# Head-norm reciprocal roots by small VectorE steps, and a Hadamard rotation moved to GpSimd, in a two-layer FFN kernel

## The chip, the cores and the metric

The kernel runs on one core of a Trainium2 chip. The metric is device time in microseconds (us) of one execution, as the median of several runs. One further execution is recorded by the hardware profiler; its page and its trace are what the readings below come from. The engines are TensorE (PE, with its weight loads PEld), VectorE (DVE), ScalarE (ACT), GpSimd (POOL) and SyncE (SP), which here only issues DMAs.

## What is computed

Two layers work on x of shape (128, 32, 256), with a condition of shape (128, 256). Cut to what matters here:

```python
# layer 0: 32 Runge-Kutta steps of a coupled system, driven by x, then an FFN with MX block quantization
def _q_w(w):                       # blocks of 32: shared power-of-two scale, then few-bit elements, at most 6
    return _quantize_mx(w, 2, 1.0, 2.0, 6.0)
...
gate = _mx_linear(x, w_gate); up = _mx_linear(x, w_up)
x = x + _mx_linear(silu(gate) * up, w_down)

# layer 1: attention with 16 heads of 16, then an FFN with rotated, quantized activations
q = q * rsqrt(mean(q * q, axis=-1) + 1e-6) * g_q          # per head
k = k * rsqrt(mean(k * k, axis=-1) + 1e-6) * g_k
attn = softmax((q @ k.T) * d ** -0.5)
...
gate, up = h_bitlinear(h, w_gate), h_bitlinear(h, w_up)   # fwht over 256, 8-bit activations, ternary weights
out = h_bitlinear(silu(gate) * up, w_down)                # fwht over 1024
```

The function fwht is a Walsh-Hadamard transform: log2(n) stages of sums and differences.

## The kernel before

The kernel has two phases. **Phase one** is layer 0. Its unit is one time step of all 128 sequences, so a tile is 128 x 256. `step` does one Runge-Kutta step: matrix products on PE, tanh and squares on ACT, multiply-adds on DVE (L513), cubes on POOL (L569). `ffn0` sends each step's state through quantization, the three MX products and a norm, some steps behind `step`. Before the first `ffn0` can multiply, six halves of weights pass through `mx_weight`: a block maximum, three small instructions for the scales (L627, L632, L639), a multiplication by the inverse scale on POOL (L688), then on DVE a clip to 6 (L692), a mask that keeps the exponent (L695), a lower bound and a factor that make a rounding constant of it (L698), its addition and subtraction, which round (L699, L700), and on POOL the multiplication by the scale (L703). The wide tiles are 128 x 1024.

**Phase two** is layer 1. Its unit is a chunk of 128 tokens, four sequences of 32; `tokens(g)` is called for 32 chunks, and up to seven are on the way at once (`behind`). One chunk does, in order: q, k and v on PE (L1043, L1050); the squares on ACT (L1059) and their sums per head on DVE (L1060); the reciprocal root of 128 x 32 means on POOL, as a multiply-add (L1063) and a power of -0.5 (L1064); the multiplications of q and k by it on DVE (L1069, L1076), and of q by the product of the gains, `g_prod`, on POOL (L1081); attention with transposes and reductions on DVE; a rotation over 256 folded into a matrix (L1151); quantization (`quantum`, L1018 to L1026); gate and up on PE (L1184), Silu on ACT (L1192), the product on DVE (L1199, two halves of 512). Then comes the rotation over 1024. Three of its ten stages, those between the eight blocks of 128 elements, are butterflies: for each stage one instruction for the sums and one for the differences (L1215), two stages on DVE and the third on POOL. The other seven stages are a matrix on PE (L1226), after a transposition (L487). A second quantization and the last product (L1249, L1256) end the chunk.

**The order** is made by a planner. Every piece of work is an item with an engine, an estimated cost, and the tiles that it reads and writes; `Work.order` plans all of them forth and back for 30 rounds from these costs, keeps the best plan, and the instructions of every engine are emitted in that order. Each engine then works through its own list in that fixed order. An item with `port=True` is not planned at the same time as another item with `port=True`: the planner takes DVE and POOL to exclude each other there. The pools of tiles (`tiny`: 24 of 128 x 32; `wide`: 8 of 128 x 1024; four single and two double PSUM banks in phase two) are shared out by the same plan. In `mx_scales` an intermediate lies in PSUM instead of SBUF; the sums of squares and the reciprocal roots lie in `tiny`, in SBUF.

Of the kernel before, what the change touches and what calls it, by code (L numbers as in the profile page):

```python
# [13 lines left out]
I32 = mybir.dt.int32  # L14
AF = mybir.ActivationFunctionType
ALU = mybir.AluOpType
AX = mybir.AxisListType
# [12 lines left out]
EXP_MASK = 0x7F800000  # L30
TINY = 2.0**-124

MAGIC = 12582912.0
HEADS = 16
D_HEAD = 16
EPS_RMS = 1e-6
EPS_QUANT = 1e-5

PE, DVE, ACT, POOL, SP = "PE", "DVE", "ACT", "POOL", "SP"

# [243 lines left out]
def kernel(  # L284
# [22 lines left out]
    nc = tc.nc  # L307
# [26 lines left out]
    mid = slots("mid", HALF, 10)  # L334
    slim = slots("slim", N, 18)
    tiny = slots("tiny", FF // BLOCK, 24)
# [38 lines left out]
    neg_half = tile_of("neg_half", [P, 2 * HEADS])  # L375
# [7 lines left out]
    add = work.add  # L383
# [294 lines left out]
    def mx_weight(w, dst, b_dst, part, rank):  # L678
        raw, rows = load_half(w, part, rank)
        nb = FF // BLOCK  # L680
        amax = Buf(tiny)
        amax_item(amax, lambda a: a, raw, lambda a: a, 1.13, rank)
        scl, inv = mx_scales(amax, nb, rank, 0.5, tiny)
        add(DVE, 0.1, lambda: nc.vector.tensor_scalar(scl.ap, scl.ap, 0.25, None, MULT), [], [scl], rank=rank)
        y, big, wq = Buf(wide), Buf(wide), Buf(wide_bf)
        add(
            POOL, 1.87,
            lambda: nc.gpsimd.tensor_tensor(blocks(y.ap), blocks(raw.ap), spread(inv.ap, BLOCK), MULT),  # L688
            [raw, inv], [y], rank=rank, port=True,
        )  # L690
        ts = nc.vector.tensor_scalar
        add(DVE, 0.6, lambda: ts(y.ap, y.ap, 6.0, -6.0, ALU.min, ALU.max), [], [y], rank=rank, port=True)  # L692

        add(
            DVE, 0.6, lambda: ts(big.ap.bitcast(I32), y.ap.bitcast(I32), EXP_MASK, None, ALU.bitwise_and),  # L695
            [y], [big], rank=rank, port=True,
        )
        add(DVE, 0.6, lambda: ts(big.ap, big.ap, 1.0, MAGIC / 2.0, ALU.max, MULT), [], [big], rank=rank, port=True)  # L698
        add(DVE, 1.135, lambda: nc.vector.tensor_tensor(y.ap, y.ap, big.ap, ADD), [big], [y], rank=rank, port=True)  # L699
        add(DVE, 1.135, lambda: nc.vector.tensor_tensor(y.ap, y.ap, big.ap, SUB), [big], [y], rank=rank, port=True)  # L700
        add(
            POOL, 1.87,
            lambda: nc.gpsimd.tensor_tensor(blocks(wq.ap), blocks(y.ap), spread(scl.ap, BLOCK), MULT),  # L703
            [y, scl], [wq], rank=rank, port=True,
        )
        turn_weight(wq, dst, b_dst, part, rows, rank)
# [68 lines left out]
    def constants_of_phase_two(rank):  # L775

        b_hf, had_ffn = load_fixed("had_ffn", [P, P], had, rank)
        b_qkv, w_qkv_sb = load_fixed("w_qkv_sb", [P, NC, 3 * N], w_qkv.rearrange("(c p) n -> p c n", p=P), rank)
        w_o = load(mid, w_out.rearrange("(c p) n -> p c n", p=P), rank, as_=two)
        b_gq, g_qk_sb = fixed("g_qk_sb", [P, 2, D_HEAD])  # L780
        for n, g in enumerate((g_q, g_k)):
            add(
                SP, 0.45, lambda n=n, g=g: nc.sync.dma_start(g_qk_sb[:, n, :], g.partition_broadcast(P)),
                fills=[b_gq], rank=rank, tail=1.8,
            )
        ts = nc.gpsimd.tensor_scalar
# [12 lines left out]
        add(  # L799
            POOL, 0.3, lambda: nc.gpsimd.tensor_tensor(g_prod, g_qk_sb[:, 0, :], g_qk_sb[:, 1, :], MULT),  # L800
            [b_gq], [b_gp], rank=rank,
        )
        add(POOL, 0.3, lambda: ts(g_prod, g_prod, 1.0, D_HEAD**-0.5, MULT, MULT), [], [b_gp], rank=rank)
        w_oT = Buf(mid)
        for m in range(NC):
            pw = Buf(ps_turn)
            add(PE, 0.22, lambda pw=pw, m=m: turn(pw.ap, two(w_o.ap)[:, m, :]), [w_o], [pw], rank=rank)
            add(
                ACT, 0.33,
                lambda pw=pw, m=m: nc.scalar.copy(two(w_oT.ap)[:, :, m * P : (m + 1) * P], two(pw.ap)),  # L810
                [pw], fills=[w_oT], rank=rank,
            )
# [16 lines left out]
        return b_hf, had_ffn, b_qkv, w_qkv_sb  # L829
# [180 lines left out]
    def heads(ap):  # L1010
        return ap.rearrange("p (h d) -> p h d", d=D_HEAD)

    def quantum(name, src, n, cost, rank):
# [14 lines left out]
        add(DVE, 0.25, scales, [], [am, sc], rank=rank)  # L1028
        return am, sc

    def tokens(g):
        rank = PHASE_TWO + g
        tok = slice(g * P, (g + 1) * P)
# [23 lines left out]
        v_pad, sq, rstd, qn, k_pad = Buf(v_pads), Buf(mid), Buf(tiny), Buf(slim), Buf(k_pads)  # L1057
        add(ACT, 0.26, lambda: nc.scalar.copy(v_pad.ap[:, :, :D_HEAD], heads(pv.ap[:, :N])), [pv], [v_pad], rank=rank)
        add(ACT, 0.477, lambda: nc.scalar.activation(sq.ap, pqk.ap, AF.Square), [pqk], [sq], rank=rank)  # L1059
        add(DVE, 0.6, lambda: nc.vector.tensor_reduce(rstd.ap, heads(sq.ap), AX.X, ADD), [sq], [rstd], rank=rank)  # L1060

        def rsqrt():
            nc.gpsimd.tensor_scalar(rstd.ap, rstd.ap, 1.0 / D_HEAD, EPS_RMS, MULT, ADD)  # L1063
            nc.gpsimd.tensor_tensor(rstd.ap, rstd.ap, neg_half, ALU.pow)  # L1064

        add(POOL, 5.65, rsqrt, [], [rstd], rank=rank)
        add(
            DVE, 0.335,
            lambda: tt(heads(qn.ap), heads(pqk.ap)[:, :HEADS, :], spread(rstd.ap[:, :HEADS], D_HEAD), MULT),  # L1069
# [261 lines left out]
```

## Time and profile before

| what | value |
|---|---|
| time, median of 3 runs | 880.15 us (878.64 to 880.85) |
| the profiled execution: time | 884.23 us |
| the profiled execution: span, first to last instruction | 882.5 us |
| mean granted PE clock | 0.956 |
| phase one, last Runge-Kutta state (L606) | 393.7 us after the span's start |
| phase two, first matmul on q and k (L1043) | about 429 us |
| phase two, first and last product of a chunk (L1199) | 474.2 and 852.3 us |
| POOL's power (L1064) | 32 instructions, 175.1 us |
| DVE's butterflies (L1215) | 128 instructions, 87.9 us |
| POOL's butterflies (L1215) | 64 instructions, 82.1 us |

How to read the lines of the profile: a group names its line in the kernel, its engine, its operation, the tile written and the tiles read, the shapes, and the count; then the busy time in us and the mean duration of one in ns, and then the idle time of the engine just before, with what ended most of it. A line of the timeline begins with the start and the duration in us; "x2" there means two instructions in a row, merged. A line of the waits says who waited for whom: us in total, times, longest.

### The profile page before, as it was taken

Reading aid. Unit: us, or ns where it says so; the run is one execution under the profiler, and the core shown is the slowest. Engines: PE = TensorE matmul, PEld = TensorE weight load, DVE = VectorE, ACT = ScalarE, POOL = GpSimd, SP = SyncE. Lnnn points to the kernel's source line nnn. Section 1 sums busy time; section 2 is a strip of 40 time slices with the busy share of each in tenths; the row PEclk is TensorE's granted clock in tenths of the full one; section 3 lists DMA queues with packets and bytes.
Section 4 is the critical chain, followed back from the end, with each engine's and each line's share of the span. In section 5 each row is a group of like instructions: output and inputs, shape, how many; then the busy total and the mean of one; then the engine's idle time right before and its main releaser. Section 6 shows DMA issues by size and latency. Waiting matters only on the chain. (4 is left out here: it accounts for less than half of the span.)

```text
span 882.5 us, 25579 instructions
## 1 busy us (share of the span) xinstructions
PE 781.6 (89%) x10300; PEld 590.1 (67%) x10300; DVE 749.4 (85%) x1885; ACT 499.3 (57%) x1014; POOL 636.4 (72%) x619
## 2 busy tenths in 40 slices
PE   7788999999999999994678989998999988988974
PEld 4566777778887887872344666866677665766654
DVE  5989999899999999998157978997989769798882
ACT  4243455555665665654324666767677647576653
POOL 5645898878899988799699649658866477766330
PEclk9989999999999999997769999999999989999997
DMA  8211332222322442425200122222122212122132
GB/s 265 66 32 42 71 77 57 71 57 67 70 73 73 106 99 65 105 65 99 47 2 15 24 45 48 64 56 56 19 56 56 55 36 56 37 54 44 47 70 66
DMA packets 128887, 55.49 MB, mean 63 GB/s; under 512 B 102144, under 2 KB 127616, under 8 KB 128768
## 3 DMA queue, kind: packets, MB, share of 16 engines
q1 hardware_dynamic: 128768, 53.85, 26.2%
q8 instruction: 81, 1.33, 0.6%
q14 instruction: 38, 0.31, 0.1%
HBM read 21.32 MB, written 8.39 MB: 34 GB/s over the span
## 5 line engine op out<-in xcount | busy, mean ns | idle before, releaser
L1064 POOL TENSOR_TENSOR tiny<-tiny,neg_half 128x32 f32<-128x32 f32 x32 | 175.1, 5472 | 2.7
L1215 POOL TENSOR_TENSOR wide<-wide 128x512 f32<-128x512 f32 x64 | 82.1, 1300 | 99.7 <-DVE wide L1215 60.8
L562 PEld LDWEIGHTS ps_stage<-slim,coup 128*128 128x128 f32 x1024 | 132.2, 194 | 14.3 <-ACT slim L555 5.2
L562 PE MATMUL ps_stage<-slim,coup 128*128 128x128 f32 x1024 | 138.9, 279 | 0.1
L569 POOL TENSOR_TENSOR slim<-slim,slim 128x256 f32<-128x256 f32 x96 | 73.6, 767 | 37.3 <-ACT slim L556 35.5
L1215 DVE TENSOR_TENSOR wide<-wide 128x512 f32<-128x512 f32 x128 | 87.9, 715 | 0.3
L548 PE MATMUL ps_stage<-drives,eye 128*128 128x256 f32 x256 | 81.2, 400 | 5.3 <-DVE ps_stage L513 3.8
L548 PE MATMUL ps_stage<-slim,eye 128*128 128x256 f32 x256 | 78.0, 394 | 7.6 <-DVE slim L513 7.6
L555 ACT ACTIVATE slim<-slim 128x256 f32<-128x256 f32 x96 | 39.5, 411 | 70.9 <-DVE slim L513 58.3
L1043 PE MATMUL ps_one<-w_qkv_sb,xnT 128*128 128x512 f32 x128 | 69.4, 671 | 2.1 <-DVE coup L1076 0.9
L917 POOL TENSOR_TENSOR wide_bf<-mid,tiny 128x512 bf16<-128x512 fp8e4 x64 | 67.7, 1064 | 3.9 <-DVE mid L841 3.7
L909 POOL TENSOR_TENSOR mid<-mid,tiny 128x512 f32<-128x512 f32 x64 | 66.3, 1049 | 4.1 <-DVE tiny L639 3.7
L1226 PE MATMUL ps_two<-had_ffn,wide 128*128 128x128 f32 x512 | 64.6, 282 | 4.3 <-DVE tiny L1025 1.6
L1226 PEld LDWEIGHTS ps_two<-had_ffn,wide 128*128 128x128 f32 x512 | 61.8, 196 | 8.4 <-DVE tiny L1025 2.1
L548 PEld LDWEIGHTS ps_stage<-slim,eye 128*128 128x128 f32 x256 | 43.5, 193 | 24.1 <-DVE slim L513 15.2
L1128 PEld LDWEIGHTS ps_one<-v_pad,mid 32*32 32x32 f32 x4096 | 42.2, 107 | 25.1 <-issue 15.5
L1199 DVE SCALAR_TENSOR_TENSOR wide<-ps_two,tiny,mid 128x512 f32<-128x512 f32 x64 | 46.5, 737 | 13.1 <-ACT mid L1192 12.9
L1128 PE MATMUL ps_one<-v_pad,mid 32*32 32x17 f32 x4096 | 47.8, 182 | 10.4 <-issue 5.9
L1192 ACT ACTIVATE mid<-ps_two,tiny 128x512 f32<-128x512 f32 x64 | 42.9, 686 | 21.9 <-PE ps_two L1184 21.0
L556 ACT ACTIVATE slim<-slim 128x256 f32<-128x256 f32 x96 | 38.9, 406 | 26.0 <-DVE slim L513 25.8
L1234 ACT ACTIVATE wide<-ps_two,magic,tiny 128x1024 f32<-128x1024 f32 x32 | 38.5, 1202 | 24.6 <-DVE tiny L1026 18.3
L548 PEld LDWEIGHTS ps_stage<-drives,eye 128*128 128x128 f32 x256 | 40.4, 195 | 14.3 <-DVE ps_stage L513 9.0
(153 smaller groups left out, 2065.7 us busy)
## 6 DMA issues: line engine op xcount, KB each, us to landing
x_step<-in_x_dram SPq DMA_DIRECT2D x32, 128.0 KB, 2.3
x_add<-in_x_dram SPq DMA_DIRECT2D x32, 128.0 KB, 2.1
x_dram<-slim SPq DMA_DIRECT2D x32, 128.0 KB, 1.7
slim<-x_dram SPq DMA_DIRECT2D x32, 128.0 KB, 2.2
out_dram<-slim SPq DMA_DIRECT2D x32, 128.0 KB, 1.7
raws<-in_L_ffn_w_gate_dram SPq DMA_DIRECT2D x4, 512.0 KB, 5.0
raws<-in_L_ffn_w_up_dram SPq DMA_DIRECT2D x4, 512.0 KB, 5.6
raws<-in_L_ffn_w_down_dram SPq DMA_DIRECT2D x4, 512.0 KB, 3.6
```

The source lines that it names most:

```text
L548: PE, cost, lambda: nc.tensor.matmul(ps[i].ap, lhsT=eyes[eye], rhs=src.ap, start=False, stop=False),
L562: nc.tensor.matmul(ps[i].ap[:, sl], lhsT=coup[i][:, c, sl], rhs=two(th.ap)[:, c, :], start=False, stop=(c == NC - 1 and m == NC - 1),)
L569: POOL, 0.685, lambda: nc.gpsimd.tensor_tensor(sq.ap, sq.ap, qi.ap, MULT),
L909: lambda it=it, ks=ks: nc.gpsimd.tensor_tensor(blocks(it.ap), blocks(it.ap), spread(binv.ap[:, ks], BLOCK), MULT),
L917: lambda b8=b8, ks=ks, sl=sl: nc.gpsimd.tensor_tensor(blocks(bq.ap[:, sl]), blocks(b8.ap), spread(bscl.ap[:, ks], BLOCK), MULT),
L1043: nc.tensor.matmul(pqk.ap, lhsT=xnT_flat[:, c, tok], rhs=w_qkv_sb[:, c, : 2 * N], start=(c == 0), stop=(c == NC - 1),)
L1064: nc.gpsimd.tensor_tensor(rstd.ap, rstd.ap, neg_half, ALU.pow)
L1128: nc.tensor.matmul(by_v(po.ap)[row, hd, :], lhsT=by_head(exT.ap)[row, hd, :], rhs=v_pad.ap[row, hd, :], start=True, stop=True,)
L1192: lambda pgu=pgu, act=act: nc.scalar.activation(act.ap, pgu.ap[:, :HALF], AF.Silu, scale=sgu.ap[:, 0:1]),
L1199: lambda pgu=pgu, act=act, sl=sl: stt(it.ap[:, sl], pgu.ap[:, HALF:], sgu.ap[:, 1:2], act.ap, MULT, MULT),
L1215: eng.tensor_tensor(dv[:, :, e, :], sv[:, :, 0, :], sv[:, :, 1, :], op)
L1226: nc.tensor.matmul(pfh.ap[:, sl], lhsT=iT.ap[:, sl], rhs=had_ffn, start=True, stop=True)
```

## The change

There are three parts.

The reciprocal root of the heads' mean squares no longer runs on POOL. A new function `rsqrt` does it in nine DVE instructions on `tiny` tiles of 128 x 32: a multiply-add, a first guess from the float's bits, and two polishing passes of three and four instructions. The result comes out with a constant factor, `RSQRT`, which `g_prod` takes out again. Each chunk uses four `tiny` tiles for this instead of one. In the planner each of the nine steps costs 0.1 and has no `port` mark.

The three butterfly stages of the rotation over 1024 all go to POOL (six instructions for each chunk instead of two).

In `mx_weight` the clip at the start goes; the mask takes one more bit by an OR in the same instruction; the first of the two rounding passes becomes a subtraction on POOL, and the second a custom DVE addition that saturates at 6 and -6 (`TENSOR_ADD_SAT`, which `step` already uses).

```diff
         ts = nc.vector.tensor_scalar
-        add(DVE, 0.6, lambda: ts(y.ap, y.ap, 6.0, -6.0, ALU.min, ALU.max), [], [y], rank=rank, port=True)
-
-        add(
-            DVE, 0.6, lambda: ts(big.ap.bitcast(I32), y.ap.bitcast(I32), EXP_MASK, None, ALU.bitwise_and),
+
+        add(
+            DVE, 0.6,
+            lambda: ts(big.ap.bitcast(I32), y.ap.bitcast(I32), EXP_MASK, 1 << 22, ALU.bitwise_and, ALU.bitwise_or),
             [y], [big], rank=rank, port=True,
         )
-        add(DVE, 0.6, lambda: ts(big.ap, big.ap, 1.0, MAGIC / 2.0, ALU.max, MULT), [], [big], rank=rank, port=True)
-        add(DVE, 1.135, lambda: nc.vector.tensor_tensor(y.ap, y.ap, big.ap, ADD), [big], [y], rank=rank, port=True)
-        add(DVE, 1.135, lambda: nc.vector.tensor_tensor(y.ap, y.ap, big.ap, SUB), [big], [y], rank=rank, port=True)
+        add(DVE, 0.6, lambda: ts(big.ap, big.ap, 1.5, 2.0**22, ALU.max, MULT), [], [big], rank=rank, port=True)
+        add(
+            POOL, 1.87, lambda: nc.gpsimd.tensor_tensor(y.ap, y.ap, big.ap, SUB), [big], [y], rank=rank, port=True
+        )
+        add(
+            DVE, 1.135,
+            lambda: nc.vector._custom_dve(TENSOR_ADD_SAT, out=y.ap, in0=y.ap, in1=big.ap, s0=6.0, s1=-6.0),
+            [big], [y], rank=rank, port=True,
+        )
...
-        add(POOL, 0.3, lambda: ts(g_prod, g_prod, 1.0, D_HEAD**-0.5, MULT, MULT), [], [b_gp], rank=rank)
+        add(POOL, 0.3, lambda: ts(g_prod, g_prod, 1.0, D_HEAD**-0.5 / RSQRT**2, MULT, MULT), [], [b_gp], rank=rank)
...
+    def rsqrt(v, y, scale, eps, rank):
+
+        t, u = Buf(tiny), Buf(tiny)
+        tt, ts = nc.vector.tensor_tensor, nc.vector.tensor_scalar
+
+        def put(fn, reads, writes):
+            add(DVE, 0.1, fn, reads, writes, rank=rank)
+
+        put(lambda: ts(v.ap, v.ap, scale, eps, MULT, ADD), [], [v])
+        put(lambda: ts(y.ap.bitcast(I32), v.ap.bitcast(I32), -0.5, float(0x5F3759DF), MULT, ADD), [v], [y])
+
+        put(lambda: tt(t.ap, y.ap, y.ap, MULT), [y], [t])
+        put(lambda: stt(t.ap, t.ap, -0.5, v.ap, MULT, MULT), [v], [t])
+        put(lambda: stt(y.ap, t.ap, 1.5, y.ap, ADD, MULT), [t], [y])
+
+        put(lambda: tt(t.ap, y.ap, y.ap, MULT), [y], [t])
+        put(lambda: stt(t.ap, t.ap, 1.0, v.ap, MULT, MULT), [v], [t])
+        put(lambda: stt(u.ap, t.ap, -10.0 / 3.0, t.ap, ADD, MULT), [t], [u])
+        put(lambda: stt(y.ap, u.ap, 5.0, y.ap, ADD, MULT), [u], [y])
...
-        def rsqrt():
-            nc.gpsimd.tensor_scalar(rstd.ap, rstd.ap, 1.0 / D_HEAD, EPS_RMS, MULT, ADD)
-            nc.gpsimd.tensor_tensor(rstd.ap, rstd.ap, neg_half, ALU.pow)
-
-        add(POOL, 5.65, rsqrt, [], [rstd], rank=rank)
+        add(DVE, 0.6, lambda: nc.vector.tensor_reduce(sq_sum.ap, heads(sq.ap), AX.X, ADD), [sq], [sq_sum], rank=rank)
+
+        rsqrt(sq_sum, rstd, 1.0 / D_HEAD, EPS_RMS, rank)
...
-        for s, engine in enumerate((DVE, DVE, POOL)):
+        for s, engine in enumerate((POOL, POOL, POOL)):
```

More of the change, by code (lines that the diff above doesn't have):

```diff
@@ L37 @@
 EPS_QUANT = 1e-5
+RSQRT = 8.0 / 3.0
 PE, DVE, ACT, POOL, SP = "PE", "DVE", "ACT", "POOL", "SP"
@@ L1056, in tokens @@
         add(PE, 0.86, v, [b_xnT, b_qkv], [pv], rank=rank, after=first, behind=behind)
-        v_pad, sq, rstd, qn, k_pad = Buf(v_pads), Buf(mid), Buf(tiny), Buf(slim), Buf(k_pads)
+        v_pad, sq, qn, k_pad = Buf(v_pads), Buf(mid), Buf(slim), Buf(k_pads)
+        sq_sum, rstd = Buf(tiny), Buf(tiny)
         add(ACT, 0.26, lambda: nc.scalar.copy(v_pad.ap[:, :, :D_HEAD], heads(pv.ap[:, :N])), [pv], [v_pad], rank=rank)
         add(ACT, 0.477, lambda: nc.scalar.activation(sq.ap, pqk.ap, AF.Square), [pqk], [sq], rank=rank)
-        add(DVE, 0.6, lambda: nc.vector.tensor_reduce(rstd.ap, heads(sq.ap), AX.X, ADD), [sq], [rstd], rank=rank)
-        def rsqrt():
-            nc.gpsimd.tensor_scalar(rstd.ap, rstd.ap, 1.0 / D_HEAD, EPS_RMS, MULT, ADD)
-            nc.gpsimd.tensor_tensor(rstd.ap, rstd.ap, neg_half, ALU.pow)
-        add(POOL, 5.65, rsqrt, [], [rstd], rank=rank)
+        add(DVE, 0.6, lambda: nc.vector.tensor_reduce(sq_sum.ap, heads(sq.ap), AX.X, ADD), [sq], [sq_sum], rank=rank)
+        rsqrt(sq_sum, rstd, 1.0 / D_HEAD, EPS_RMS, rank)
         add(
```

## The prediction, made before the change was run

> **What bounds the kernel now.** I read the busy line first, then the busy time by stage, then the costliest groups, then the timeline where DVE and POOL meet. The busy line names PE and DVE together, so no single engine is the answer:
>
> ```profile
> PE 781.6 (89%) x10300; PEld 590.1 (67%) x10300; DVE 749.4 (85%) x1885; ACT 499.3 (57%) x1014; POOL 636.4 (72%) x619
> ```
>
> By stage (columns: stretch in us, its length, then busy us of PE, weight load, DVE, ACT, POOL, the granted PE clock, DMA):
>
> ```profile
> 14.00:92.00 78.00, 63.77 (x348) 47.23 (x348) 71.52 (x171) 28.27 (x75) 44.76 (x41) 0.93 0.26 70
> 92.00:429.00 337.00, 312.88 (x2056) 248.06 (x2054) 309.81 (x868) 192.31 (x542) 296.40 (x393) 0.97 0.34 78
> 429.00:480.00 51.00, 39.70 (x781) 24.67 (x782) 29.32 (x64) 16.22 (x29) 43.21 (x20) 0.80 0.03 7
> 480.00:850.00 370.00, 339.28 (x6976) 250.81 (x6975) 316.98 (x742) 244.79 (x342) 239.02 (x137) 0.98 0.22 47
> 850.00:882.50 32.50, 18.05 (x119) 14.38 (x117) 14.65 (x28) 12.07 (x12) 5.71 (x4) 0.80 0.28 67
> ```
>
> The first stretch holds the MX weights beside the first Runge-Kutta steps: DVE 71.5 of 78 us. In the second, DVE (92%) and POOL (88%) are both nearly full. In the third, phase two fills its pipeline; POOL is busiest, 43.2 of 51 us. The fourth is phase two at its pace, 370 us: PE 92%, DVE 86%, POOL 65%. The change touches the first stretch and the last three. Its objects are these groups:
>
> ```profile
> L1064 POOL TENSOR_TENSOR tiny<-tiny,neg_half 128x32 f32<-128x32 f32 x32 | 175.1, 5472 | 2.7
> L1215 POOL TENSOR_TENSOR wide<-wide 128x512 f32<-128x512 f32 x64 | 82.1, 1300 | 99.7 <-DVE wide L1215 60.8
> ...
> L1215 DVE TENSOR_TENSOR wide<-wide 128x512 f32<-128x512 f32 x128 | 87.9, 715 | 0.3
> ```
>
> POOL's power takes 5.47 us for each chunk of phase two; the rotation takes DVE four instructions and POOL two. The last thing to read is what one engine does to the other:
>
> ```profile
> 584.71 2.94 POOL L1215 TENSOR_TENSOR wide<-wide 128x512 f32<-128x512 f32 x2 [7.42 <-DVE wide L1215]
> ...
> 585.51 2.69 DVE L1215 TENSOR_TENSOR wide<-wide 128x512 f32<-128x512 f32 x2
> ```
> ```profile
> 410.31 1.13 POOL L917 TENSOR_TENSOR wide_bf<-mid,tiny 128x512 bf16<-128x512 fp8e4 x1
> ...
> 410.77 0.68 DVE L724 TENSOR_TENSOR tiny<-tiny 128x1 f32<-128x1 f32 x1
> ```
> ```profile
> 623.42 5.44 POOL L1064 TENSOR_TENSOR tiny<-tiny,neg_half 128x32 f32<-128x32 f32 x1
> ...
> 624.89 1.28 DVE L1215 TENSOR_TENSOR wide<-wide 128x512 f32<-128x512 f32 x2
> ```
>
> Two DVE butterflies beside POOL butterflies take 2.69 us; beside POOL's power they take 1.28. And a DVE addition of one element per row (L724, both inputs in SBUF) lasts 0.68 us, ending at 411.45, just when POOL's instruction ends (410.31 + 1.13 = 411.44). So a tiny DVE instruction with two SBUF inputs waits out a POOL multiplication, while the power, long as it is, does not keep DVE out.
>
> [...] here two 128x32 TENSOR_SCALARs (L639, L632) start 0.10 us apart (411.37, 411.47). [...] here 1.27 against 0.68 us at the median (L1215), 1.9 times.
>
> **The change part by part.** The sum is made against the profiled execution, 884.2 us with 882.5 of span; it lies 4.1 above the median of 880.15, and I carry the difference over to the median.
>
> Rotation to POOL. In 480 to 850, 118 DVE butterflies go. In the chain of waits two in a row take 1.20 us, so 0.60 each: 71 us, and some 2 of port waits: DVE 317 - 73 = 244. POOL gets four more per chunk at 1.27: 5.1 us.
>
> Power to small steps. POOL loses 5.47 + 0.24 (L1063) = 5.7 us per chunk, so in all POOL stays level at about 0.76 + 6 x 1.27 = 8.4 us per chunk. DVE gets nine instructions of 128x32 for each of the 25 chunks whose power starts after 480: 225 in all. Independent ones cost 0.10; dependent ones lie 0.18 apart (L1025 to L1026), but other DVE work can go between; I take 0.12, 27 us (bounds 22 and 40). Without any port wait DVE has 244 + 27 = 271.
>
> The port. What POOL did for 5.7 us without shutting DVE out becomes work that does. POOL now holds the port for 6 x 1.25 + 0.73 (g_prod) = 8.2 us per chunk of some 12.2 (L1199's first and last starts, 474.2 and 852.3, over 31 chunks), 67% of the time. Seven of the nine new steps read two SBUF inputs, and the other two are SBUF-to-SBUF TENSOR_SCALARs (L684, of that shape, took 0.17 alone and 0.22 where a POOL instruction ended just then). DVE takes its instructions in order: behind a waiting small step stand the reductions, transposes and butterfly inputs of other chunks, and PE and ACT wait for those. An arrival at random waits 0.67 x 0.62 = 0.42 us; a step right behind one that waited meets the next butterfly of a run, but outside a run several pass freely, and a slower pace thins POOL's share. I take **0.34 us**, bounds 0.1 and 0.55. That is 225 x 0.34 = 76 us: DVE 347.
>
> Pace. DVE's share today is 317/370 = 0.857: 347/0.857 = 405. Part of today's idle time is the wait for the power, which goes:
>
> ```profile
> DVE slim L1069 <- POOL tiny L1064: 11.3, 9, 3.0
> ```
>
> 405 - 11 = 394, against 370: **+24 us**. Next late are DVE's own port waits.
>
> Filling (429 to 480). Seven powers stand in a row on POOL there, 5.7 to 7.2 us between starts; the first runs from 434.85, and its chunk's DVE multiplication follows at 441.05. Nine dependent steps at 0.2 us are about 1.8, and no butterfly runs yet. Chunk 0 would be 4 us earlier, the next ones a little more, but PE is busy 39.7 of the 51 us at a clock of 0.80: **-5** (0 to -10).
>
> MX weights. Per half-weight, DVE loses the clip (0.60 from start to next start) and one of two 128x1024 passes (1.13: L700 starts at 36.48, the next at 37.61): 1.73 x 6 = 10.4 us. The added OR rides in an existing instruction, and the saturating addition takes the time of the plain one, for which POOL gets one pass of 1.91 (L703's and L688's row), 11.5 us in all. POOL has room, 44.8 of 78 us, but the chain now goes DVE, POOL, DVE, POOL, and behind the new pass wait the cubes of the Runge-Kutta steps (L569). **-6** (bounds -10 and +4). No DMA is added or moved, and SP's queue is the same.
>
> Draining (after 850). The last chunks' rotation takes POOL 7.6 us each in place of DVE's 2.4 and POOL's 2.5. The last chunk alone is 2.7 longer, and POOL may not have finished the one before: **+4** (2 to 8).
>
> Sum: 24 - 5 - 6 + 4 = +17, or 901 for the profiled execution, **897** at the median. The planner writes a new order of everything, which I leave at nothing (5 either way).
>
> **The rivals.**
> *Faster: the port hardly matters (0.1 us per step).* The planner might place the steps in POOL's gaps, or a 32-element read might slip in. For it: the power shows that not every POOL instruction keeps DVE out. Against it: all three L724 run to a POOL instruction's end. Then DVE has 271 + 22 = 293 and PE bounds: 339 us at 95% is 357, -13. With -5, -6 and +2: -22, **858**.
> *Balance.* (271 + 225w)/0.857 - 11 = 377, which the other parts' -7 cancel, gives w = 0.27 us per step: 880. Above this point the kernel is slower, below it faster. My value is not far above it.
> *Much slower: runs of butterflies catch nearly every step* (0.55 us). DVE 271 + 124 = 395, pace 450, +80 - 7: **953**. For it: at 585 two DVE butterflies in a row lost 1.4 us to POOL. Against it: POOL has only seven such instructions per chunk.
>
> **How the numbers follow.** A run of this kernel can be told from no change beyond about 0.3%, 2.6 us. Forecast 0.56 (its own range 883 to 925), faster 0.24, balance 0.07, much slower 0.13. So faster 0.24, same 0.07, slower 0.69. The range of 862 to 940 leaves out about half of the faster case below and 0.08 above.
>
> **What would show it.** Right: DVE's small steps with means well above 0.2 us and maxima near 1.3, ending with POOL butterflies; DVE's busy time in phase two up though 128 butterflies left it; first q-multiplication some 4 us sooner after its reduction; steps of 13 us in the first 100 us shortened. Wrong: small steps at 0.1 to 0.2 us throughout, DVE's share in phase two falling to three quarters, PE at 95%. A late first stage, or a long drain behind POOL, would make single terms wrong.

## The result, and the profile after

| | before | after |
|---|---|---|
| median, 4 runs each | 880.5 us (878.6 to 884.4) | 931.5 us (929.9 to 932.7) |
| ratio, 95% interval | | 1.057 [1.053, 1.061] |
| profiled execution: time, span | 884.2, 882.5 us | 929.9, 928.1 us |
| phase two: first matmul on q and k; length | 429.6; 452.9 us | 442.8; 485.3 us |

Slower by 51 us at the median, where +17 was forecast. The profiled executions lie 45.7 us apart; the other 5 are scatter of single executions. In the trace the loss has two places: phase two begins 13.2 us later, and it is 32.4 us longer.

The whole of phase two, before and after (stretch in us, its length, then busy us of PE, weight load, VectorE, ScalarE and POOL, the granted PE clock, DMA):

```profile
429.60:882.50 452.90, 397.01 (x7872) 289.84 (x7872) 360.94 (x832) 272.56 (x382) 287.94 (x160) 0.94 0.20 44
```
```profile
442.80:928.10 485.30, 407.89 (x7872) 298.65 (x7872) 378.40 (x998) 278.72 (x388) 261.18 (x224) 0.92 0.20 43
```

The busy line of the page, after:

```profile
PE 795.6 (86%) x10300; PEld 600.1 (65%) x10300; DVE 760.8 (82%) x2033; ACT 504.8 (54%) x1020; POOL 619.7 (67%) x689
```

The busy time by stage, in the columns of the prediction, with the stretches moved to where the same work lies now:

```profile
14.00:105.00 91.00, 74.72 (x415) 55.02 (x415) 84.16 (x216) 31.73 (x85) 72.31 (x67) 0.94 0.27 69
105.00:439.00 334.00, 304.99 (x1989) 240.74 (x1986) 291.87 (x805) 185.85 (x526) 276.89 (x372) 0.96 0.32 74
439.00:490.00 51.00, 40.31 (x914) 26.08 (x915) 41.57 (x136) 18.56 (x34) 6.89 (x9) 0.84 0.08 17
490.00:895.00 405.00, 352.13 (x6858) 260.71 (x6856) 329.48 (x848) 251.53 (x351) 241.77 (x206) 0.94 0.21 44
895.00:928.00 33.00, 16.09 (x104) 12.44 (x104) 7.75 (x18) 11.46 (x11) 12.52 (x11) 0.77 0.25 56
```

In the fourth stretch, phase two at its pace, every engine's share has fallen: PE from 92% to 87%, VectorE from 86% to 81%. No engine became the bound, and yet the stretch is longer. That is the puzzle of this case. PE, the busiest, also got a lower granted clock, 0.94 for 0.98 in this stretch; over phase two it is busy 11 us longer with the same 7872 matmuls.

The line numbers are now those of the changed kernel: L1239 is the butterfly (L1215 before), L1223 the product of gate and up (L1199), L1093 the multiplication of q by the root (L1069), L1105 that by the gains on POOL (L1081), and L1046 to L1056 are the small steps. The groups. First POOL's butterflies, now all six of a chunk, and three of VectorE's nine small steps:

```profile
L1239 POOL TENSOR_TENSOR wide<-wide 128x512 f32<-128x512 f32 x192 | 238.7, 1270 | 88.7 <-DVE wide L1223 76.7
```
```profile
L1047 DVE TENSOR_SCALAR tiny<-tiny 128x32 int32<-128x32 int32 x32 | 16.7, 522 | 0.3
L1049 DVE TENSOR_TENSOR tiny<-tiny 128x32 f32<-128x32 f32 x32 | 14.6, 456 | 0.4
...
L1056 DVE SCALAR_TENSOR_TENSOR tiny<-tiny,tiny 128x32 f32<-128x32 f32 x32 | 7.4, 231 | 0.6
```

All 288 small steps together take 102.5 us: median 0.19, longest 1.26, 67 of them over 0.25. The timeline shows where the long ones end:

```profile
624.97 3.71 POOL L1239 TENSOR_TENSOR wide<-wide 128x512 f32<-128x512 f32 x3
625.36 0.92 DVE L1049 TENSOR_TENSOR tiny<-tiny 128x32 f32<-128x32 f32 x1
626.31 1.19 DVE L1050 SCALAR_TENSOR_TENSOR tiny<-tiny,tiny 128x32 f32<-128x32 f32 x1
627.53 1.19 DVE L1051 SCALAR_TENSOR_TENSOR tiny<-tiny,tiny 128x32 f32<-128x32 f32 x1
628.76 0.19 DVE L1053 TENSOR_TENSOR tiny<-tiny 128x32 f32<-128x32 f32 x1
...
629.44 0.19 DVE L1056 SCALAR_TENSOR_TENSOR tiny<-tiny,tiny 128x32 f32<-128x32 f32 x1
```

Three steps end with the three butterflies of the run; the four steps behind it take 0.19 each. Of all 67 long steps, 63 end within 0.06 us of the end of a butterfly, and the other four so with L1105. While one of the 67 ran, no other VectorE instruction began until 0.084 us or less before its end. I call the part of a step over 0.19 us its port wait: 50.4 us in all. "Port" is the planner's word (`port=True`); what the trace shows is that the ends fall together.

The wait for POOL's power was 11.3 us before. Its successor in the waits (500 to 850 us), and the largest of VectorE's waits there:

```profile
DVE wide L1223 <- ACT mid L1216: 18.1, 16, 3.3
...
DVE slim L1093 <- DVE tiny L1056: 0.2, 1, 0.2
```

Phase one: I find the late start of phase two in three places. The first interval between Runge-Kutta states is 18.3 us (13.6 before). Work of the MX part stands in it: the new pass on POOL (L701), forecast at 1.91 us, takes 2.4 to 3.3, and a small VectorE step (L685) that stands ahead of the state's last instruction ends 1.7 us late, with such a pass. The one before the 25th state is 18.6 (12.0 before): in SyncE's list (SPq) three loads of 512 KB for layer 1 stand just ahead of a transposition, and PE waits for it:

```profile
294.88 0.43 SPq L406 DMA_DIRECT2D raws<-in_L_ffn_w_gate_dram  x1
299.73 0.33 SPq L944 DMA_DIRECT2D x_dram<-slim  x1
300.11 0.43 SPq L406 DMA_DIRECT2D raws<-in_L_ffn_w_gate_dram  x1
300.59 0.56 SPq L406 DMA_DIRECT2D raws<-in_L_ffn_w_up_dram  x1
301.25 2.39 SPq L396 DMA_TRANSPOSE wide_bf<-wide_bf  x1
```
```profile
308.74 1.89 PE L936 MATMUL ps_po<-w0dT,wide_bf 128*128 128x256 bf16 x8 [4.16 <-DMA wide_bf<-wide_bf]
```

And at the end, PE holds its first q and k matmul back for two statistics of a ternary weight that ScalarE makes last (L725), though the last xnT tile is done at 439.61:

```profile
439.02 0.59 ACT L971 COPY xnT<-ps_turn 128x256 f32<-128x256 f32 x1 [0.84 <-PE ps_turn L488]
439.41 1.05 ACT L725 ACTIVATE wide<-raws 128x1024 f32<-128x1024 f32 x1
...
441.83 0.59 PE L737 MATMUL ps_turn<-tiny,ones 128*128 128x1 f32 x2 [2.85 <-DVE tiny L731]
...
442.76 2.05 PE L1070 MATMUL ps_one<-w_qkv_sb,xnT 128*128 128x512 f32 x2 [0.34 <-DVE wscale L743]
```

None of the instructions shown for phase one is in the diff. They stand there because the planner wrote a new order.

### The profile page after: what moved, and what is told of

It is laid out like the page before. It is cut to its first block, busy times and chain, and to the rows that moved or that the text cites. A ratio compares the mean times of both kernels' runs of the same rounds, so it can differ in the third digit from the quotient of the medians.

```text
span 928.1 us, 25818 instructions
## 1 busy us (share of the span) xinstructions
PE 795.6 (86%) x10300; PEld 600.1 (65%) x10300; DVE 760.8 (82%) x2033; ACT 504.8 (54%) x1020; POOL 619.7 (67%) x689
## 4 chain that ended last, share of the span: by engine, by line
PE 43%; DVE 34%; POOL 7%; ACT 6%; issue 5%; DMA 4%; SPq 0%; DVEq 0%; ACTq 0%; POOLq 0%
PE ps_stage L549 8%; PE ps_stage L563 8%; PE ps_two L1250 4%; PE ps_two L1208 4%; PE ps_gu L889 3%; PE ps_one L1070 3%; DVE tiny L1025 3%; DMA wide_bf<-wide_bf 3%; PE ps_one L1122 2%; DVE ps_sum L514 2%; PE ps_po L936 2%; PE ps_turn L488 2%; PE ps_one L1273 2%; DVE slim L514 2%; DVE wide L1223 2%
## 5 line engine op out<-in xcount | busy, mean ns | idle before, releaser
L1239 POOL TENSOR_TENSOR wide<-wide 128x512 f32<-128x512 f32 x192 | 238.7, 1270 | 88.7 <-DVE wide L1223 76.7
L1105 POOL TENSOR_TENSOR slim<-slim,g_prod 128x256 f32<-128x256 f32 x32 | 23.2, 726 | 119.9 <-DVE slim L1093 104.3
L570 POOL TENSOR_TENSOR slim<-slim,slim 128x256 f32<-128x256 f32 x96 | 70.1, 730 | 39.4 <-ACT slim L557 36.1
L549 PE MATMUL ps_stage<-slim,eye 128*128 128x256 f32 x256 | 75.5, 389 | 5.9 <-DVE slim L514 5.7
L1250 PE MATMUL ps_two<-had_ffn,wide 128*128 128x128 f32 x512 | 70.5, 297 | 7.1 <-DVE wide L1223 3.8
L1250 PEld LDWEIGHTS ps_two<-had_ffn,wide 128*128 128x128 f32 x512 | 67.0, 210 | 12.0 <-DVE wide L1223 4.6
L1070 PE MATMUL ps_one<-w_qkv_sb,xnT 128*128 128x512 f32 x128 | 63.6, 625 | 5.4 <-DVE slim L1093 2.2
L1223 DVE SCALAR_TENSOR_TENSOR wide<-ps_two,tiny,mid 128x512 f32<-128x512 f32 x64 | 47.2, 744 | 24.8 <-ACT mid L1216 24.5
L557 ACT ACTIVATE slim<-slim 128x256 f32<-128x256 f32 x96 | 38.9, 406 | 30.1 <-DVE slim L514 29.1
L1208 PE MATMUL ps_two<-w1gT,slim_bf 128*128 128x512 bf16 x128 | 40.7, 401 | 13.5 <-ACT wide L1258 5.6
L1208 PEld LDWEIGHTS <-slim_bf 128*128 128x128 bf16 x256 | 24.6, 101 | 41.6 <-issue 16.9
```

The source lines that it names most:

```text
L549: PE, cost, lambda: nc.tensor.matmul(ps[i].ap, lhsT=eyes[eye], rhs=src.ap, start=False, stop=False),
L570: POOL, 0.685, lambda: nc.gpsimd.tensor_tensor(sq.ap, sq.ap, qi.ap, MULT),
L1070: nc.tensor.matmul(pqk.ap, lhsT=xnT_flat[:, c, tok], rhs=w_qkv_sb[:, c, : 2 * N], start=(c == 0), stop=(c == NC - 1),)
L1208: nc.tensor.matmul(pgu.ap[:, n * HALF : (n + 1) * HALF], lhsT=two(aT.ap)[:, c, :], rhs=w[:, sr, c, :], start=(c == 0), stop=(c == NC - 1),)
L1223: lambda pgu=pgu, act=act, sl=sl: stt(it.ap[:, sl], pgu.ap[:, HALF:], sgu.ap[:, 1:2], act.ap, MULT, MULT),
L1239: eng.tensor_tensor(dv[:, :, e, :], sv[:, :, 0, :], sv[:, :, 1, :], op)
```

## The experiments

In the diffs, the base is the changed kernel unless another is named. "Phase two" is the time from the first q and k matmul to the end of the span, in the profiled execution.

The theories. *Port*: what costs is the small steps' waits for POOL, one for one. *VectorE's time*: any time added in VectorE's list costs as much, waits or not. *Order*: it costs because the emitted order was planned without it; planned with it, it costs little; and phase one's 13 us are the order too. *MX part*: its POOL passes delay phase one, the last half-weight above all (its last pass starts at 107.7 us instead of 90.3).

### One part at a time

e1 takes the kernel before and the MX part alone.

> The kernel before with the MX part alone. In the changed kernel the last of the six half-weights is finished at 107.7 us (90.3 before), though the fifth is done 12 us sooner than before, and phase two starts 13 us later. Theory L (the planner puts the last half late once the MX part is lighter, and the first down product of layer 0 waits for it): the last half again after 100 us, phase two's first matmul 8 to 13 us later than before's 429.6, 888 to 894 us in all. The forecast's own step (-6): 874. Rival O (no part costs anything by itself, the changed kernel merely drew a poor order): within 5 us of 880.

Measured: 875.7 us, ratio 0.9975 [0.996, 0.999]. Its last half-weight is as late (the pass starts at 112.0), but phase two starts at 427.9. The MX part is worth -2.4 us against the 878.15 of before in this batch, and the late half costs nothing that shows.

e2 takes the kernel before and the small steps alone: power out, rotation on two engines as before.

> The kernel before with the reciprocal roots on DVE alone; the rotation stays with four instructions on DVE and two on POOL. [...] Theory P (what the small steps lose, they lose to POOL's butterflies): small steps 0.19 us of duration and a port wait of 0.05 to 0.1 each, a third of the changed kernel's; DVE keeps its butterflies, so its load in phase two is 317 + 27 + some 15 = 360 us, at the share of 0.86 some 30 more with the power's waits taken off: 900 to 915. Rival O: the cost is in the order and not in these parts: 875 to 890. Rival F (the long POOL power was the real brake of phase two): 860 to 872.

Measured: 896.0, 1.018 [1.014, 1.022], between the figures of the first two theories. Phase two is 463.2 us with VectorE at 405 of them; port waits 16 us, 30 steps over 0.25. The phase starts at 430.9, so phase one is hardly touched.

e3 is the changed kernel with the old MX part.

> The changed kernel with the old MX part: roots on DVE and rotation on POOL. Theories L and P together: phase one as before (first matmul of phase two near 430 us), phase two as in the changed kernel (485 us): 914 to 922. If the MX part cost nothing by itself (rival O): 925 to 935, or anywhere, with phase two as different from 485 as the new order makes it.

Measured: 950.6, 1.079 [1.074, 1.084]. Without the MX part, phase two starts still later, at 446.3 (this time the third Runge-Kutta interval is 21.3 us). So the MX part does not make phase one late. Phase two is 502 us with nearly the same port waits (55.8): the order alone moves it by more than 10.

e10 takes small steps and MX part, with the rotation as before.

```diff
-        for s, engine in enumerate((POOL, POOL, POOL)):
+        for s, engine in enumerate((DVE, DVE, POOL)):
```

> The small steps and the MX part together, the rotation as before (two stages on VectorE, one on POOL); nothing is left out. If the parts add up: 896.0 (small steps alone) - 2.4 (MX alone) = 893.6 us, first phase as before at 428 to 431 us, small steps with about 16 us of waits over 190 ns; then the rotation's move is worth 931.5 - 893.6 = +38, nearly all of it the 34 us of port waits that it adds. If the planner's new order is what costs (the first phase of the changed kernel was 13 us longer and so was that of small steps with rotation but without MX), any combination can fall out of line: 885 or 910, and the rotation's share can't be read from it.

Measured: 900.2, 1.024 [1.020, 1.027], 7 over the sum of the parts. Phase two is 456.7, but starts at 440.2, although each part alone started it at 428 to 431. The rotation's move therefore costs some 31 us, 29 of them in phase two.

### The port

e4 leaves the rotation out: the butterflies become powers of six columns, meant to occupy POOL as long without holding VectorE, as the power of the kernel before did.

```diff
-                    eng.tensor_tensor(dv[:, :, e, :], sv[:, :, 0, :], sv[:, :, 1, :], op)
+                    few = slice(e, e + 901, 180)
+                    eng.tensor_tensor(dst.ap[:, few], src.ap[:, few], ones[:, :6], ALU.pow)
```

> The changed kernel in the same planned order, but each of POOL's butterflies is a power on 6 columns of the tile in place of a sum on 512: the rotation over 1024 is left out. In the kernel before the power of 32 columns did not keep DVE out; 6 columns should take about 1.3 us by the two lengths seen there (0.55 us for 1, 5.44 for 32), as long as a butterfly. Theory P: small steps at 0.19 us with maxima near 0.25, the 53 us of port waits gone from DVE, and 30 to 50 us of the 931 with them: 880 to 900. Rival O (the order is poor, the waits hide in idle time): 920 to 931 although the port waits are gone.

Measured: 881.1, 1.002 [1.000, 1.005]. The powers take 1.32 us at the median, the butterflies 1.27. Port waits fall from 50.4 to 2.7 us, VectorE's busy time in phase two from 378 to 330, and phase two by 47 us:

```profile
444.90:883.00 438.10, 392.31 (x7872) 289.38 (x7872) 330.27 (x998) 278.15 (x388) 270.62 (x224) 0.95 0.22 47
```

In this order the waits are paid one for one. Phase one is as in the changed kernel (444.9), so the late start has nothing to do with the rotation's execution.

e6 tells the planner that the steps use the port, and nothing else.

```diff
-            add(DVE, 0.1, fn, reads, writes, rank=rank)
+            add(DVE, 0.1, fn, reads, writes, rank=rank, port=True)
```

> The changed kernel with port=True on each small step, so that the planner keeps them and POOL's butterflies apart; the instructions are the same. Theory P: port waits nearly gone (small steps at 0.19 us at the median and on the mean below 0.23), phase two 15 to 30 us shorter than 485, 900 to 916 in all. Rival (keeping apart costs what waiting did, since POOL's free gaps are few): 925 to 940.

Measured: 894.4, 1.020 [1.016, 1.024]: 37 us less, more than either figure said, though the waits are not nearly gone: 35.4 us are left, 15 fewer. Phase two starts at 435.4. The instructions are the same, so what the waits don't explain is the new order too.

e7 keeps one operand of each step in PSUM, in the v bank, which takes twelve steps and leaves the other products three banks.

```diff
-    ps_one = [Slot(None, f"one{i}") for i in range(4)]
+    ps_one = [Slot(None, f"one{i}") for i in range(3)]
+    ps_v = [Slot(None, "v0")]
...
-        put(lambda: tt(t.ap, y.ap, y.ap, MULT), [y], [t])
+        put(lambda: tt(t.ap, y.ap, yp(), MULT), [y, pv], [t])
```

> The changed kernel with the small steps' second operand in PSUM: the guess and the polished values are written twice, to PSUM and to SBUF, so that no step reads two SBUF tiles; 12 steps in place of 9. They lie in the free half of the bank of v, which is then held until the root is done, and the other products share three banks in place of four. Nothing is left out. Theory P: no step beyond 0.25 us, 885 to 905. Rival (the bank that is missing holds up PE as much as the port held up DVE): 915 or more.

Measured: 887.1, 1.011 [1.006, 1.016]; the longest step is 0.200 us. The longest of the changed kernel is 1.261. So with one operand in PSUM not one of the 384 steps waited for POOL, though all 192 butterflies ran there.

### The late loads

e8 leaves the six ternary weight loads of phase one out (the weights are made from what lies there).

```diff
-            SP, 0.45, lambda: nc.sync.dma_start(as_(b.ap) if as_ else b.ap, src),
+            SP, 0.45, lambda: None if skip else nc.sync.dma_start(as_(b.ap) if as_ else b.ap, src),
```

> The changed kernel without the DMAs that load the ternary weights in phase one (six of 512 KB; the weights are then made from what lies in the tiles). In the changed kernel three of them are issued from 294.9 to 300.6 us, and the transposition of an activation tile issued at 301.25 lands 7.45 us later (3.1 at the median); PE waits for it and one Runge-Kutta step takes 18.6 us in place of 11.5. Theory D (the loads delay the transposition): that step at 11 to 12 us, phase one and the whole 5 to 8 us shorter, 923 to 927. Rival (another cause in the order): no change, 931.

Measured: 926.9, 1.056 [1.052, 1.061]. The interval before the 25th state falls from 18.6 to 13.1 us, and phase two starts 5.0 earlier. The kernel before has these loads too, and 12.0 us there; so the loads, where they now stand in SyncE's list, are 5 of the 13 us.

### Waits, or VectorE's time?

e5 is e4 with a fill of 110 columns behind every small step.

```diff
+            def both():
+                fn()
+                nc.vector.memset(junk, 0.0)
...
-            add(DVE, 0.1, fn, reads, writes, rank=rank)
+            add(DVE, 0.1, both, reads, writes, rank=rank)
```

> The kernel without port waits of the run before (power in place of the butterflies, rotation left out), with a plain DVE memset of 110 columns behind each of the 288 small steps, which the planner does not know of: about 0.175 us each, 50 us in all, as much as the port waits of the changed kernel took, but spread evenly. Theory A (phase two pays for any DVE time that is not in the plan, however it comes): 40 to 50 us more than without, 920 to 930. Rival B (it pays for the long single waits of 1 to 1.2 us that hold up the rest; small even delays vanish in DVE's idle time of some 100 us in phase two): 10 to 25 more, 890 to 905.

Measured: 885.7, 1.011 [1.005, 1.017]. Under both figures, since the dose was not the one meant: VectorE's busy time rose by 14 us only (344 for 330). Consecutive small steps start 0.24 us apart, against 0.22 in e4, though the fill lasts 0.15. These 14 us, of which the planner does not know either, made phase two 1.3 us longer in the profiled executions and the kernel 4.6 at the median: a small dose was not paid in full.

e9 is the same with 260 columns.

> The changed kernel's plan with the rotation left out (its twelve POOL butterflies become powers over six columns, as in the run without port waits, 881.1 us), and now a VectorE fill of 260 columns behind every small step. A fill of 110 columns took 150 ns and one of a single column 59 ns, so 0.83 ns a column and 275 ns for 260; in the run with 110 columns a step and its fill together took 0.235 us from start to start, so here 0.36 us, about 0.17 us more than a bare step, 288 times: some 50 us, the same sum as the port waits of the changed kernel, but in equal small pieces. Theory one (what is paid is VectorE's time as such): VectorE's busy time in phase two rises from 330 to about 380 us and the time from 881 to 920 to 930. Theory two (the waits cost so much because they come as single ones of up to 1.26 us in the middle of a chain that TensorE waits for, or because something else of the butterflies is paid): VectorE is as busy, but the time stays between 883 and 900.

Measured: 924.4, 1.050 [1.047, 1.053]. No port waits (1.6 us), but VectorE is busy 46 us more than in e4, and phase two is 42 longer:

```profile
442.50:922.70 480.20, 405.76 (x7872) 294.29 (x7872) 376.04 (x1286) 278.48 (x388) 271.00 (x224) 0.93 0.20 43
```

So in this order it is VectorE's time that is paid. That it came as port waits does not matter.

e13 moves that time behind the chunk's last addition, for which only the store waits (rotation left out, as in e4): two fills of 830 columns.

```diff
+            nc.vector.memset(junk, 0.0)
+            nc.vector.memset(junk, 0.0)
```

> The changed kernel's plan with the rotation left out (881.1 us without delay), and the VectorE time that the fills behind the small steps took (46 us, which made 924.4 us of it) put in another place: once per chunk, behind the last addition of the chunk, which nothing but the store of the output waits for, two fills of 830 columns, 59 + 829 x 0.83 = 0.75 us each, 48 us in all. If it is the time in VectorE's queue that is paid, wherever it stands: 918 to 930. If it is paid because the root chain is what TensorE waits for: 881 to 895.

Measured: 923.4, 1.052 [1.048, 1.056].

```profile
442.80:919.20 476.40, 404.11 (x7872) 295.53 (x7872) 374.54 (x1062) 278.31 (x388) 270.73 (x224) 0.93 0.20 43
```

44 us of VectorE time, 38 us of phase two: the place does not matter much either, and the root chain's latency is not needed to explain the price.

### Told or not told

e15 is e9 with the truth told to the planner (the base is e9).

```diff
-            add(DVE, 0.1, both, reads, writes, rank=rank)
+            add(DVE, 0.36, both, reads, writes, rank=rank)
```

> The kernel with a fill of 260 columns behind every small step and the rotation left out (924.4 us), with 0.36 us told to the planner for a step and its fill instead of 0.1. Order theory: 885 to 900. Theory that VectorE's time is paid in any order: 915 to 930.

Measured: 886.3, 1.011 [1.007, 1.014].

```profile
431.80:883.60 451.80, 397.51 (x7872) 291.27 (x7872) 369.32 (x1280) 278.69 (x388) 270.48 (x224) 0.94 0.21 46
```

The instructions are those of e9, and so is the rotation left out; only one figure of the planner differs, and 38 us are gone: 28 in phase two and 11 ahead of it. VectorE still has 39 us more to do than in e4; phase two pays 14. So its time is not paid in any order. How much of the 38 comes from the true figure and how much from merely having another order, one pair cannot say: e3's phase two was planned from the changed kernel's figures and is 17 us longer.

e14 tells the changed kernel's planner 0.35 for each step.

> The changed kernel, nothing left out, with 0.35 us instead of 0.1 told to the planner for each small step (they took 0.356 on average): only the order changes. If the order that doesn't know of the waits is what makes them dear, the new one puts other work in front and the time falls to 885 to 905 (declaring the steps as users of the port gave 894). If the time on VectorE is what is paid in any order: 922 to 940; the planner itself then ends later by about as much.

Measured: 929.9, 1.060 [1.056, 1.064]. No gain, and this one I missed. Phase two starts earlier (436.2), but port waits rose from 50.4 to 77.0 us and phase two to 490.8:

```profile
L1047 DVE TENSOR_SCALAR tiny<-tiny 128x32 int32<-128x32 int32 x32 | 17.4, 544 | 0.2
L1051 DVE SCALAR_TENSOR_TENSOR tiny<-tiny,tiny 128x32 f32<-128x32 f32 x32 | 16.6, 519 | 0.2
```

Here a port wait was no constant that could be told: for the same instructions the sum was 50.4 us in one order, 35.4 in another (e6) and 77.0 in this one.

e17 tells both, the port and 0.19 us for the bare step.

> The changed kernel, nothing left out; only the planner's figures differ: each small step is declared as a user of the port and as 0.19 us (0.1 and no port in the changed kernel; the declaration alone, at 0.1, gave 894.4 with 35 us of waits left). Order theory: with 26 us of VectorE time less that the planner doesn't know of, 870 to 885. Theory that the declaration's gain came only from fewer waits: 890 to 900.

Measured: 899.4, 1.022 [1.019, 1.025], outside the order theory's figure and inside its rival's. Phase two is 450.2, 7 less than in e6 at nearly the same waits (31.8), but it starts 13 later, at 448.6. Told the true cost, the kernel did not gain; phase one, with the same instructions, came out longer.

### Back to a version that pays

e11 and e12 take the twelve-step PSUM form of e7 with one, and with two, of the rotation's stages back on VectorE.

```diff
-        for s, engine in enumerate((POOL, POOL, POOL)):
+        for s, engine in enumerate((DVE, POOL, POOL)):
```

> The changed kernel with the twelve-step form that keeps one operand in PSUM (887.1 us, no step over 250 ns), and the first of the rotation's three stages back on VectorE; nothing is left out. Theory 'TensorE bounds once the waits are gone': 128 butterflies more on VectorE, 0.6 us each, 38 us in two halves; VectorE's busy time in phase two goes from 349 to about 385 us, and POOL's from 261 to some 175; with VectorE's slack of 100 us in a phase of 455 this gives 882 to 892, no visible change. Theory 'VectorE paces': +0.4 to 0.8 of the 38 us: 902 to 917.

Measured: 897.9, 1.022 [1.018, 1.025]; VectorE 384 us, phase two 465.6. Between the two figures.

> Small steps in PSUM and the MX part, the rotation's two first stages on VectorE as before; nothing is left out. It is the sum of small steps and MX with their port waits taken out. If waits are paid one for one here too: 893.6 - 16 = 877 to 878, plus three steps more per chunk (96 x 0.18 = 17 us of VectorE time), of which between nothing and all is paid: 877 to 895. If this lies under 875.7 (MX alone) it is the version that beats both kernels; on the theory that VectorE's 405 us of busy time pace the small-step kernel, it stays at 890 or over.

Measured: 894.5, 1.015 [1.010, 1.019]; VectorE 408 us, phase two 463.0. Giving the rotation back gains nothing over e7 (887.1); the intervals of e7 and e12 overlap, so they are not told apart.

e16 rewrites the steps so that nine suffice with one operand in PSUM (sp, tp and wp lie there). One polishing pass of it:

```diff
...
+        put(lambda: stt(tp(), sp(), eps, y.ap, ADD, MULT), [y], [pv])
+        put(lambda: stt(wp(), tp(), -0.5, y.ap, MULT, MULT), [y], [pv])
+        put(lambda: stt(y.ap, wp(), 1.5, y.ap, ADD, MULT), [pv], [y])
...
```

> The whole change with the steps rewritten so that each has one operand in PSUM and there are nine instead of the twelve of the earlier PSUM form (887.1 us); the sum of squares goes to PSUM directly, and the factor 1/16 into the constant of the gammas; nothing is left out (the seed of the root leaves the epsilon aside, the refinements have it). 96 steps of 0.18 us less are 17 us of VectorE time. If VectorE's time in this chain is paid one for one: 887 - 17 = 870 us, phase two 438 as in the run with the rotation left out, and it beats both kernels and MX alone (875.7). If the 438 us came from the rotation being left out: 880 to 887.

Measured: 884.1, 1.008 [1.005, 1.011]; phase two 448.6. It is 3 us under e7, not 17, and inside the rival's figure: my one-for-one price, carried over to another order, failed here. (VectorE has 15 us less to do than in e7, and phase two is 7 shorter.)

e18 is e16 with 0.19 told instead of 0.1.

> The nine-step PSUM form (884.1), nothing left out, with 0.19 us instead of 0.1 told to the planner, which is what a step takes there (188 ns, no waits): 25 us of VectorE time that it didn't know of are now in its sum. Order theory: some 5 to 20 us less, 864 to 879, and under 875 it beats both kernels and MX alone. If the remaining 10 us of phase two over the run without rotation (448.6 against 438.1) are the rotation on POOL itself: 880 to 887.

Measured: 876.0, 0.997 [0.995, 0.999].

```profile
430.20:873.60 443.40, 390.52 (x7872) 285.95 (x7872) 336.78 (x998) 287.17 (x394) 260.76 (x224) 0.97 0.23 47
```

The same instructions as e16, 8 us less. With the same idea and the same split of engines as the change, this kernel is 0.3% under the one before, at the edge of what can be told. MX alone (e1) is as fast, and e18 contains it: so roots and rotation bring nothing of their own in the best form tried here.

## Why the prediction was right or wrong

**The direction was right, and so was the kind of wait.** Small steps whose inputs lie in SBUF waited out POOL's butterflies; the longest took 1.26 us, and 63 of the 67 long ones end with a butterfly. That goes for the two TENSOR_SCALARs with one input as well (L1047: 522 ns in the mean). Where fewer butterflies ran on POOL there were fewer waits (e2, 64 for 192: 16 us for 50.4), and none where one operand was in PSUM (e7: no step over 0.200 us).

**The step that failed** is the last sentence of its sum: the planner's new order, "which I leave at nothing (5 either way)". It was worth more than the forecast's total: the same instructions in another order, e6, take 37 us less. The prediction itself held a reason not to leave it at nothing. It priced a step at 0.12 + 0.34 = 0.46 us, while the change tells the planner 0.1 and no port; the order was planned without three quarters of that. The order failed the forecast in two ways.

*Ahead of phase two.* Forecast -6 (MX), measured +13.2: 19 of the 29 us by which the profiled executions' sum was missed (45.7 against 17). The MX part by itself is -2.4 (e1), so its sign was right and its size under half; its new POOL pass took 2.37 us at the median, not 1.91 (the saturating addition, L705, took 1.22 as the plain one, L700, had taken 1.21, and the mask 0.68 with the OR as without), and the first Runge-Kutta interval, which was to be shorter, is longer. The rest is order. The changed kernel, e6, e14 and e17 hold the same instructions and differ in the planner's figures for phase two alone; their phase two starts at 442.8, 435.4, 436.2 and 448.6. Of the 13, 5 are the loads (e8), shown; the first interval and the late statistics are read from the trace alone, and their shares stay open.

*In phase two.* Forecast +24 - 5 + 4 = +23, measured +32.4. The sum was near for a wrong reason, the **pace** step, which netted the waits against the relief and divided by VectorE's share. Its terms, against the runs:

| term | forecast | measured |
|---|---|---|
| a step without port wait | 0.12 us | 0.18 us (median of e4); dependent steps 0.22 us from start to start |
| port wait of a step | 0.34 us (225 steps, 76 us) | 0.175 us (288 steps, 50.4 us) |
| what the waits add to the time | netted, then divided by 0.857 | 47 us of 47.7 (e4) |
| without port waits | paced stretch 65 us shorter (271/0.857 - 11 = 305 for 370) | phase two 15 us shorter (438.1 for 452.9); the rival with PE as the bound had -13 for the paced stretch |

The 0.12 supposed that other work would stand between dependent steps. In e4 a step follows directly on the one whose result it reads 111 times, 0.22 us after it. Small steps of two chunks side by side (23 pairs) do start about 0.10 apart, as the prediction had it for independent ones; but the pair that it read this from (L639, L632) reads PSUM and not SBUF.

VectorE's time was not one currency. With 79 us less of it (phase two of e10 against e4: 409 to 330) phase two was 19 us shorter; the two differ in order too, and that PE, with 392 of the 438 us to do, bounds there is my reading. Adding 44 to 48 us that the order was not made for cost 38 to 47, as port waits (changed kernel), as fills in the root chain (e9) or at the chunk's end (e13), while VectorE had over 100 us of idle time in phase two. Planned, 39 us cost 14 (e15), and the small dose of e5, 14 us unplanned, cost 1 to 5. That the order decides is shown.

The traces show where the loss arrives, added up over phase two:

| | e4 | changed kernel | e9 | e13 | e15 |
|---|---|---|---|---|---|
| PE's waits for VectorE and ScalarE, us | 15 | 47 | 49 | 46 | 27 |
| ScalarE's waits for VectorE, us | 59 | 101 | 93 | 95 | 63 |
| PE's busy time, us | 392 | 408 | 406 | 404 | 398 |
| granted PE clock | 0.95 | 0.92 | 0.93 | 0.93 | 0.94 |

Of the 47 us between e4 and the changed kernel, 32 are waits of PE, and 16 are PE's own longer busy time for the same matmuls at a lower granted clock. Whether the clock fell because PE stood still more often was not tried, so the cause of this third of the loss stays open. Nor is it shown why an order that doesn't know of the delay turns so much of it into waits. I can only argue: VectorE's idle time stands in front of instructions that wait for PE and ScalarE (50.6 of the 51.1 us that VectorE's waits list from 500 to 850 us), and these are behind by the same delay.

The **balance** point of 0.27 us per step was wrong with the pace: at 0.175 the kernel lost 51 us.

**Filling** (-5): chunk 0's q multiplication came 8.6 us after its first matmul instead of 11.5, 3 sooner and not 4, but its first product 43.9 instead of 44.6 us after. It gave 0.7 us. **Draining** (+4): last product to the end 32.5 instead of 30.1, +2.4.

What stays open: why e16's phase two is 10 us longer than e4's. The rotation that e4 leaves out, the PSUM bank and the order all differ. How much of a gain like e15's comes from the true figure, and how much from merely having another order, is open too: told the bare step's cost, e18 gains 8 us on e16, while e14, told 0.35, and e17 gain nothing. And no figure told to the planner made the changed kernel's own steps as cheap as the PSUM form (best 894.4).

## What to carry to other kernels

In a kernel whose engines run lists that were planned from costs, a new operation's cost in the plan is part of the change: check it against the first profile, and expect that time which was not planned can be paid nearly in full even on an engine that is a fifth idle (here 44 to 48 us were, 14 us were not). VectorE's wait for POOL could not be planned as a constant here (e14: 50.4 us became 77.0); take the operand elsewhere (here one of two to PSUM: no step over 0.200 us) and tell the true cost of what is left. When a change alters an order written by a planner, keep ten microseconds or more in the range for work that the diff doesn't name, and look for it there first.

## What the runs showed of the hardware

POOL's power did not shut VectorE out, even in the middle of a row of them: with all 192 butterflies made powers of six columns (e4), 6 of the 288 small steps were over 0.25 us, against 67, and all six end with POOL's multiplication by the gains (L1105), which e4 keeps. Dependent 128x32 steps took 0.18 to 0.19 us each and started 0.22 apart, independent ones about 0.10 (e4); but a fill behind each of them cost less than its own length: 110 columns lasted 0.150 us and moved the next start by some 0.02 (0.24 us apart in e5); 260 columns lasted 0.275 us and moved it by 0.17 (e9). So the dose here is the busy time that was added, 14 us in e5 and 46 in e9, and not the 43.2 and 79.2 us that the fills themselves lasted.
